# Linear attention and edge maps on one core: queries, keys and values in one pass over x, and plain heads divided in the projection out

## The chip, the cores and the metric

One NeuronCore of a Trainium2 chip runs the whole program in one launch. The metric is the device time in microseconds (us) from start to end. The engines are TensorE (PE, matmuls; its weight loads are PEld), VectorE (DVE), ScalarE (ACT), GpSimd (POOL) and SyncE (SP). Transfers run on 16 DMA engines, and are issued by SP's queue and by POOL's queue, each in order. On-chip memory is SBUF (128 partitions) and PSUM, which holds matmul results in eight banks of 128 x 512 float32.

## What is computed

Two layers on x of 4 images x 512 channels x 64 x 64 points, all in float32. The first is a linear attention over 64 heads of 8 channels, on the plain projections and again on their convolved copy:

```python
def layer0(x):                                     # cut to what matters
    q, k, v = h @ wq.T, h @ wk.T, h @ wv.T         # h: x with channels last
    qkv = ...                                      # per head 8 q, 8 k, 8 v channels
    dw = conv5x5_depthwise(qkv); pw = conv1x1_grouped(dw)
    qkv_all = concatenate([qkv, pw], axis=1)       # 64 plain heads, 64 convolved ones
    query, key_ = relu(f[:, :, :d]), relu(f[:, :, d:2*d])
    value_pad = concatenate([value, ones])         # the ones make the denominator
    scores = einsum('bhdn,bhen->bhde', value_pad, key_)
    out = einsum('bhde,bhen->bhdn', scores, query)
    out = out[:, :, :-1] / (out[:, :, -1:] + EPS)
    y = conv1x1(out, proj_kernel)                  # 1024 -> 512 channels
    return batch_norm(y) + x
```

The second takes four edge maps of its input with 3x3 kernels (Sobel, Laplace, diagonal, gradient), mixes each with a 512 -> 128 matmul, batch norm and GELU, weighs the 512 channels by a small attention over their means, mixes them 512 -> 512, applies a layer norm over channels and GELU, and adds its input.

## The kernel before

**Groups and strips.** The first layer goes through 16 groups: 4 images (b) x 4 groups (g) of 128 channels. An image's points are 8 strips of 512, in two halves of four. `load_x` (L265) brings a strip in two pieces of 512 KB on SP's queue; image 0 stays in SBUF, from image 1 on a group takes the strips from a pool of 8 pieces (`xst`).

**Two passes.** `keys_and_values` projects keys (`project`, L274) and values (`values`, L305) strip by strip, turns the keys (`turn`, L331) and sums the scores (`scores`, L342, added up on DVE in `s_sb`, L350). `queries` then reads the strips again, from the two that are still there, and projects the queries. `project` copies the result on ACT (`strip`, L283) and, for keys and queries, stores it from POOL's queue to a DRAM buffer `flat` (L288), of which there are two per kind; for queries ACT also makes `rq`, the relu (L281).

**Plain heads.** For each half of a group `denominators` multiplies `rq` with the key sums (`den`, L387), `invert` makes the reciprocal on DVE (`rec`, L380 and L381), `spread_out` spreads it over the channels with four matmuls into four banks (`over`, L396), and `divide` multiplies on DVE (L404) and stores `heads` to DRAM (SP).

**Convolved heads.** `roll` brings `flat` back with its rows rearranged (`rolled`, L295, POOL's queue, into one buffer). `convolve` (L418) makes a half's 5x5 convolution with 160 matmul instructions into four banks, 80 into the first two and then 80 into the others; ACT reads the banks, for keys in two pieces each, with relu and a sum (L431), for queries whole (L437). `conv_turn` (L445, L447) turns the convolved keys. `correlate` (L473) multiplies them with shifted values that are read back from DRAM (`near`: stored in `values`, L318, loaded by `load_near`, L458, into three buffers); four calls 0 to 3 fill two banks, and `weigh` (DVE, L491, L492), called at the end of the last, empties them. `conv_denominators` (`cden`, L565), `spread_out` and `conv_divide` (L574) end in `cheads` in DRAM. What of this a group doesn't reach in its own passes is done in the next group's first pass.

**PSUM.** Eight banks in two kinds of four: `ps_tile` (projections, values, turns, denominators, `yps`) and `quad_tiles` (convolution, correlation, `over`), each taken in the order in which the program asks.

**The image behind.** Three stages of the previous image run between the steps of the current one: Y (`project_out`), which reads `hd` (the plain heads of a strip, 1 MB, L656) and four `chd` (convolved heads, 256 KB each, L660), both on SP's queue, multiplies both with folded weights (`yps`, L676, first the four products with `hd`, then those with `chd`), adds shift and x (`yt`, L681) and stores `y`; E (`edge_branches`), with the edge maps on DVE, ACT and POOL and the matmuls `br` (L753); and F (`fuse_out`, `zps`, L865). `advance` hands each step of a pass a share of them, by hand-set shares and a pace. After the last group come a tail of its remaining steps with shares of their own, and then the last image's stages ("left").

PE's order is the program's; the other engines' orders are made by a scheduler from the same program.

Of the kernel before, what the change touches and what calls it, by code (L numbers as in the profile page):

```python
# [50 lines left out]
KV_ORDER = (1, 0, 2, 3, 4, 5, 6, 7)  # L51
Q_ORDER = (6, 7, 5, 4, 3, 2, 1, 0)
# [28 lines left out]
WORK, VALS = 18, 3  # L81
# [8 lines left out]
def conv_seq_kernel(  # L90
# [11 lines left out]
    xst = front.enter_context(tc.tile_pool(name="xst", bufs=8))  # L102
# [30 lines left out]
    def const_col(name, value):  # L133
# [12 lines left out]
    flats = {  # L146
        (t, n): dram.tile([4, P, NB, W], F32, name=f"flat{t}{n}", bufs=1) for t in (KEY, QUERY) for n in range(2)
    }

    def flat_border(n):  # L150

        for t in (KEY, QUERY):
            for r in range(4):
                nc.gpsimd.dma_start(out=flats[t, n][r, :, 0 if r < 2 else NB - 1, :], in_=zero_row[:, 0, 0:W])
# [64 lines left out]
    zero_row = const.tile([P, NCH, WB], F32, name="zero_row")  # L219
# [10 lines left out]

    class Group:


        def __init__(self, b, heads, cheads, folded, g):
            self.b, self.heads, self.cheads, self.folded, self.g = b, heads, cheads, folded, g
            self.near_dram = near[(NG * b + g) % 2]
            self.w, self.mat = {}, {}
            self.strip, self.rq, self.held, self.conv, self.near, self.rolled = {}, {}, {}, {}, {}, {}
            self.flat = {t: flats[t, (NG * b + g) % 2] for t in (KEY, QUERY)}
            self.nears = iter([(half, jp, b) for half in range(2) for jp in range(2) for b in range(2)])  # L240
# [3 lines left out]
        def load_w(self, t):  # L244
            self.w[t] = gw.tile([P, NCH, P], F32, name="w_sb", tag="w_sb", bufs=3)
            nc.sync.dma_start(out=self.w[t], in_=wqkv[self.g, t])
# [13 lines left out]
        def load_x(self, j):  # L260
            xs[self.b, j] = []
            for n in range(2):
                pool = x_first if self.b == 0 and j not in Q_ORDER[:2] else xst
# [4 lines left out]
        def project(self, t, j):  # L268
# [8 lines left out]
            if t == QUERY and (self.g == NG - 1 or self.b and j not in KV_ORDER[:2]):  # L277
                del xs[self.b, j]
            if t == QUERY:
                self.rq[j] = work_tile("rq")  # L280
                nc.scalar.activation(self.rq[j], ps, AF.Relu)  # L281
# [18 lines left out]
        def values(self, j):  # L300
# [8 lines left out]
            if self.b and j not in Q_ORDER[:2]:  # L309
                del xs[self.b, j]  # L310
            vt = vts[KV_ORDER.index(j) % 3]
# [16 lines left out]
        def turn(self, j):  # L328
# [5 lines left out]
            self.held[j] = kt, vts[KV_ORDER.index(j) % 3]  # L334
            del self.strip[j]

        def scores(self, j):
# [8 lines left out]
            if j == KV_ORDER[0]:  # L346
# [4 lines left out]
            if j == KV_ORDER[-1]:  # L351
                self.ks = mini.tile([P, 32], F32, name="ks_sb")
# [25 lines left out]
        def invert(self, den):  # L378
            rec = work_tile("rec")
            nc.vector.tensor_scalar(rec, den, ATT_EPS, None, ALU.add)  # L380
            nc.vector.reciprocal(rec, rec)  # L381
            return rec

        def denominators(self, half):
            den = ps_tile("den")
            for k in range(4):
                nc.tensor.matmul(  # L387
                    den[32 * k : 32 * k + 32, :], lhsT=self.ks, rhs=self.rq[4 * half + k], start=True, stop=True
                )
            self.rec = self.invert(den)  # L390

# [6 lines left out]

        def divide(self, half):
            banks = self.spread_out(self.rec)  # L400
            for k in range(4):
                j = 4 * half + k
                q = work_tile("q")
                nc.vector.tensor_mul(q, self.rq.pop(j), banks[k])  # L404
                nc.sync.dma_start(out=self.heads[j, :, self.g, :], in_=q)
# [170 lines left out]

        def keys_and_values(self, before):

# [558 lines left out]
```

## Time and profile before

| | us |
|---|---|
| three runs | 4784.38 median, 4782.71 to 4795.94 |
| the profiled execution | 4783.19, its span 4781.4 |
| PE busy in image 0's groups (0 to 840) | 806.67 |
| PE busy from 840 to 4080 | 3078.29 of 3240 |
| PE busy in the tail and the last image's stages (4080 to 4781) | 623.67 of 701 |
| mean granted clock of PE in the three stretches | 0.99, 0.98, 0.93 |
| DMA busy share in the three stretches | 0.82, 0.79, 0.53 |
| bytes moved | 997.96 MB, mean 209 GB/s |

The profile is one execution. The page gives each engine's busy time and a row of forty equal slices of the span (digits are tenths). The view of waits lists, for each line of an engine, how long the engine stood idle before it, and which instruction or transfer ended that: `yps L676 <- DMA chd` means that PE stood before a product of line 676 until a chd load had landed. Windows give the busy time of each engine between two times, with PE's granted clock (1.00 is full) and the share of time for which the 16 DMA engines were busy. The timeline lists the instructions of an engine in order of time, with the idle time before each.

The costliest transfers of the page (count, KB each, median us from issue to landing): x 316 x 512, 7.5; near loads 256 x 528, 9.6; rolled 512 x 256, 7.1; flat 256 x 256, 5.9; heads 128 x 256, 5.4; chd 128 x 256, 8.3; hd 32 x 1024, 7.7.

### The profile page before, as it was taken

To read this page: it belongs to the slowest core of one execution; us is meant where nothing else is said; L and a number is where in the kernel's file an instruction comes from. 1 tells how busy PE (TensorE), PEld (TensorE's weight loads), DVE (VectorE), ACT (ScalarE), POOL (GpSimd) and SP (SyncE) were. 2 spreads that over 40 slices of the span, in tenths; PEclk is the share of its full clock that TensorE was granted. 3 is DMA by queue.
4 is the path that set the end of the run, shared out by engine and by line. 5 is a ranking of instruction groups with operands and counts; after the bars stand their busy time and mean duration, and the time that the engine had idled before them with its cause. 6 is when DMAs were issued, how large, how long until landed. Compare 5 with 4: busy or idle time off the path is not lost. (4 is left out here: it accounts for less than half of the span.)

```text
span 4781.4 us, 85619 instructions
## 1 busy us (share of the span) xinstructions
PE 4508.6 (94%) x35900; PEld 2454.5 (51%) x35900; DVE 2102.4 (44%) x2788; ACT 1589.2 (33%) x2719; POOL 986.1 (21%) x1291
## 2 busy tenths in 40 slices
PE   8999999998999999989999999998999999899987
PEld 5555554444656554444465656453446565434433
DVE  1222222114666624311356654441125667347966
ACT  2122121002555423300244453430014545214765
POOL 2111111111121123211112121441111211111443
PEclk9999999999999999999999999999999999999998
DMA  9777799757898977877589888679668887655435
GB/s 258 176 181 193 184 257 255 180 158 196 230 248 230 264 220 216 241 185 193 166 227 259 225 259 238 213 228 226 168 187 235 236 239 202 206 161 152 152 129 174
DMA packets 466289, 997.96 MB, mean 209 GB/s; under 512 B 185544, under 2 KB 218344, under 8 KB 443376
## 3 DMA queue, kind: packets, MB, share of 16 engines
q1 hardware_dynamic: 383728, 722.41, 54.4%
q0 software_dynamic: 82176, 270.07, 20.6%
q8 instruction: 283, 4.64, 0.4%
q14 instruction: 102, 0.84, 0.1%
HBM read 710.67 MB, written 281.61 MB: 208 GB/s over the span
## 5 line engine op out<-in xcount | busy, mean ns | idle before, releaser
L274 PE MATMUL proj<-xt,w_sb 128*128 128x512 f32 x2048 | 947.1, 606 | 20.7 <-DVE s_sb L350 9.6
L274 PEld LDWEIGHTS proj<-xt,w_sb 128*128 128x128 f32 x2048 | 379.7, 193 | 507.9 <-issue 446.2
L418 PE MATMUL cv<-rolled,mat 64*32 64x504 f32 (+2 forms) x10240 | 574.5, 594 | 30.4 <-DMA rolled<-flat 14.1
L676 PE MATMUL yps<-chd,fold_sb 128*128 128x512 f32 x1024 | 470.8, 600 | 51.8 <-DMA chd<-cheads 51.7
L865 PE MATMUL zps<-ef,wf_sb 128*128 128x512 f32 (+1 forms) x1056 | 469.8, 598 | 28.5 <-ACT z L870 16.3
L305 PEld LDWEIGHTS val<-w_sb,xt 128*128 128x128 f32 x4096 | 469.7, 192 | 42.7 <-issue 29.5
L305 PE MATMUL val<-w_sb,xt 128*128 128x128 f32 x4096 | 484.9, 277 | 1.7 <-DVE vt L312 1.2
L676 PE MATMUL yps<-hd,fold_sb 128*128 128x512 f32 x1024 | 467.7, 600 | 10.1 <-DMA hd<-heads 8.5
L681 DVE SCALAR_TENSOR_TENSOR yt<-yps,shift,xr 128x512 f32<-128x512 f32 x128 | 95.7, 749 | 841.6 <-PE yps L676 726.4
L753 PE MATMUL br<-maps,wbr_sb 128*128 128x256 f32 (+1 forms) x1792 | 463.5, 412 | 0.0
L753 PEld LDWEIGHTS br<-maps,wbr_sb 128*128 128x128 f32 x1792 | 334.7, 189 | 137.4 <-issue 96.7
L418 PEld LDWEIGHTS cv<-rolled,mat 64*32 64x32 f32 x10240 | 196.9, 108 | 376.2 <-issue 353.7
L295 POOL DMA_DIRECT2D rolled<-flat x512 | 273.3, 538 | 537.3 <-PE cv L418 493.2
L288 POOL DMA_DIRECT2D flat<-strip x256 | 144.9, 566 | 1152.2 <-ACT strip L283 1117.9
L283 ACT COPY strip<-proj 128x512 f32<-128x512 f32 x256 | 149.1, 582 | 676.5 <-PE proj L274 676.3
L676 PEld LDWEIGHTS yps<-chd,fold_sb 128*128 128x128 f32 x1024 | 194.6, 192 | 304.6 <-issue 232.6
L473 PE MATMUL corr<-near,ckt 128*32 128x160 f32 x8192 | 331.9, 315 | 18.3 <-DMA near<-near 16.9
L865 PEld LDWEIGHTS zps<-ef,wf_sb 128*128 128x128 f32 x1056 | 203.6, 196 | 277.8 <-issue 226.5
L676 PEld LDWEIGHTS yps<-hd,fold_sb 128*128 128x128 f32 x1024 | 192.8, 192 | 248.9 <-issue 243.9
L473 PEld LDWEIGHTS corr<-near,ckt 128*32 128x32 f32 x8192 | 256.7, 111 | 114.2 <-issue 53.7
L685 POOL DMA_DIRECT2D y<-yt x128 | 114.4, 894 | 958.7 <-DVE yt L681 787.3
L729 DVE TENSOR_TENSOR maps<-dv 128x1054 f32<-128x1054 f32 (+1 forms) x112 | 159.9, 1428 | 257.0 <-PE br L753 256.9
(133 smaller groups left out, 4711.6 us busy)
## 6 DMA issues: line engine op xcount, KB each, us to landing
xt<-in_x SPq DMA_DIRECT2D x316, 512.0 KB, 7.5
near<-near SPq DMA_DIRECT2D x256, 528.0 KB, 9.6
rolled<-flat POOLq DMA_DIRECT2D x512, 256.0 KB, 7.1
flat<-strip POOLq DMA_DIRECT2D x256, 256.0 KB, 5.9
win<-y SPq DMA_DIRECT2D x96, 396.0 KB, 5.8
near<-vt SPq DMA_DIRECT2D x512, 66.0 KB, 5.6
y<-yt POOLq DMA_DIRECT2D x128, 264.0 KB, 6.1
heads<-q SPq DMA_DIRECT2D x128, 256.0 KB, 5.4
```

Of the source, the lines that this page charges most:

```text
L274: nc.tensor.matmul(ps, lhsT=self.w[t][:, c, :], rhs=xs[self.b, j][c], start=(c == 0), stop=(c == NCH - 1))
L283: nc.scalar.copy(s, ps)
L288: nc.gpsimd.dma_start(out=self.flat[t][r, :, b : b + 8, :], in_=rows(s))
L295: nc.gpsimd.dma_start(out=self.rolled[t, half][r::8, :, :], in_=self.flat[t][r % 4, :, at : at + 8, :].rearrange("(n c) b w -> c n (b w)", ...
L305: nc.tensor.matmul(ps[:, ts(c, P)], lhsT=xs[self.b, j][n][:, ts(c, P)], rhs=self.w[VALUE][:, n, :], start=(n == 0), stop=(n == NCH - 1),)
L418: nc.tensor.matmul(rows(banks[2 * s + i])[32 * j : 32 * j + 32, :, c0:c1], lhsT=self.mat[t][q, 4 * s + j, (dx + 2) * 4 : (dx + 2) * 4 + 4, :],
L473: nc.tensor.matmul(self.banks[jj][32 * i : 32 * i + 32, 160 * b : 160 * b + 160], lhsT=self.held["c", i][:, at : at + 32], rhs=v[:, 4 * n ...
L676: nc.tensor.matmul(ps, lhsT=fold_sb[g // NG][:, g % NG, ts(c, P)], rhs=hd[g], start=(g == 0), stop=(g == 2 * NG - 1),)
L685: nc.gpsimd.dma_start(out=y[c, :, at : at + 29 : 4, :], in_=yt)
L729: nc.vector.tensor_sub(flat[:, half : 3 * half - 2], dvs[:, 2 : 2 * half], dvs[:, 0 : 2 * half - 2])
L753: nc.tensor.matmul(rows(ps), lhsT=wbr_sb[:, k, c, :], rhs=rows(maps[:, slot[k], c % 2, :], WB)[:, :, 0:W], start=(c == 0), stop=(c == NCH ...
L865: nc.tensor.matmul(ps, lhsT=wf_sb[:, k, ts(c, P)], rhs=ef[k], start=(k == 0), stop=(k == 3))
```

## The change

**One pass.** `keys_and_values` and `queries` go. `steps` makes a group's 24 steps: for each strip the key projection, the value projection with its turn, and the query projection with its scores. The order of strips and of halves alternates with the group's parity, so that a group starts with the two strips that the one before ended with. All that a group needs beyond its projections, the two key convolutions included, is in `rest`, and is done in the next group's pass, at fixed steps. The previous image's stages are added at step 21 of the next image's first group; before, behind its first pass.

**Plain heads.** `rq`, `denominators`, `divide` and `heads` go. The queries' `flat` is kept for a whole image (two images in turn), and `project_out` loads `hd` from it, in rows of 2 KB instead of 8. `attend` makes, for the strip to come, the relus (ACT), the denominators of the four groups and their reciprocal, and two by two the spread and the product, with `over` in `ps` banks. The four products with `chd` go first. A strip's loads are issued before the products of the one before.

**Buffers.** Work tiles 18 to 16, x pieces 8 to 7, projection weights 3 to 6, `chd` 6 on the right and 4 for the last image's stages. The last group's remaining steps are `rest` with a table of shares, where step 8 stands before step 7.

```diff
-KV_ORDER = (1, 0, 2, 3, 4, 5, 6, 7)
-Q_ORDER = (6, 7, 5, 4, 3, 2, 1, 0)
+ORDERS = ((1, 0, 2, 3, 4, 5, 6, 7), (6, 7, 5, 4, 3, 2, 1, 0))
-WORK, VALS = 18, 3
+WORK, VALS = 16, 3
...
+    flat_k = [dram.tile([4, P, NB, W], F32, name=f"flatk{n}", bufs=1) for n in range(2)]
+    flat_q = [dram.tile([NG, 4, P, NB, W], F32, name=f"flatq{n}", bufs=1) for n in range(2)]
...
+            self.order, self.halves = ORDERS[g % 2], (g % 2, 1 - g % 2)
...
-            if t == QUERY:
-                self.rq[j] = work_tile("rq")
-                nc.scalar.activation(self.rq[j], ps, AF.Relu)
...
-        def denominators(self, half):
-            den = ps_tile("den")
-            for k in range(4):
-                nc.tensor.matmul(
-                    den[32 * k : 32 * k + 32, :], lhsT=self.ks, rhs=self.rq[4 * half + k], start=True, stop=True
-                )
-            self.rec = self.invert(den)
...
-        def divide(self, half):
-            banks = self.spread_out(self.rec)
-            for k in range(4):
-                j = 4 * half + k
-                q = work_tile("q")
-                nc.vector.tensor_mul(q, self.rq.pop(j), banks[k])
-                nc.sync.dma_start(out=self.heads[j, :, self.g, :], in_=q)
...
+            return {
+                1: [cv(KEY, h0), roll(KEY, h1)],
+                2: [*ct([(h0, 0), (h0, 1)]), own("fold_turn")],
+                3: ct([(h0, 2), (h0, 3)]),
+                4: [*co(h0, 0, 0), own("fold")],
+                5: co(h0, 0, 2),
+                6: co(h0, 1, 0),
+                7: [cv(KEY, h1), roll(QUERY, h0)],
+                8: co(h0, 1, 2),
+                9: [*ct([(h1, 0), (h1, 1)]), own("conv_sums")],
+                10: [*ct([(h1, 2), (h1, 3)]), own("load_pc", t=0.0)],
+                11: co(h1, 0, 0),
+                12: co(h1, 0, 2),
+                13: [cv(QUERY, h0), roll(QUERY, h1)],
+                14: co(h1, 1, 0),
+                15: [*co(h1, 1, 2), own("conv_denominators", h0), own("mix")],
+                16: [own("conv_weights")],
+                17: [own("conv_divide", h0), own("conv_heads")],
+                18: [cv(QUERY, h1), own("conv_fold")],
+                19: [own("conv_denominators", h1)],
+                21: [own("conv_divide", h1)],
+            }
...
+            own = {
+                8: [one(0.0, "load_mat", KEY)],
+                12: [(0.0, lambda: [following.load_w(t) for t in (KEY, VALUE, QUERY)])] if following else [],
+                16: [one(0.0, "load_wtab")],
+                19: [one(0.0, "load_mat", QUERY), one(0.0, "roll", KEY, self.halves[0])],
+                20: [one(0.0, "load_near", VALS)],
+            }
+            other = before.rest() if before else {}
+            if before and not self.g:
+                own[21] = [(0.0, lambda: behind.extend(stages(before)))]
+            seq = []
+            for i, j in enumerate(self.order):
+                for n, made in enumerate((
+                    [one(T_PROJ, "project", KEY, j)],
+                    [one(T_PROJ, "values", j), one(T_TURN, "turn", j)],
+                    [one(T_PROJ, "project", QUERY, j), one(T_SCORES, "scores", j)],
+                )):
+                    seq += made + other.get(3 * i + n, []) + own.get(3 * i + n, [])
+            return seq
...
+                r, at = (k + 2) % 4, 8 * half + (k + 2) // 4
+                q = pool.tile([P, NG, 512], F32, name="hd", tag="hd", bufs=2)
+                nc.sync.dma_start(
+                    out=q, in_=flat_q[b % 2][:, r, :, at : at + 8, :].rearrange("g p b w -> p g (b w)")
+                )
+                hd = [q[:, g, :] for g in range(NG)]
-                    t = pool.tile([P, 512], F32, name="chd", tag="chd", bufs=6)
+                    t = pool.tile([P, 512], F32, name="chd", tag="chd", bufs=6 if side == "right" else 4)
...
+            def attend(hd, part):
+                if part == 0:
+                    for g in range(NG):
+                        nc.scalar.activation(hd[g], hd[g], AF.Relu)
+                    den = ps_tile("den")
+                    for g in range(NG):
+                        nc.tensor.matmul(den[32 * g : 32 * g + 32, :], lhsT=ks[g], rhs=hd[g], start=True, stop=True)
+                    recs[:] = [pool.tile([P, 512], F32, name="hrec", tag="hrec")]
+                    invert(recs[0], den)
+                    return
+                for g in (2 * part - 2, 2 * part - 1):
+                    q = slice(32 * g, 32 * g + 32)
+                    over = ps_tile("over")
+                    nc.tensor.matmul(over, lhsT=spread[q, :], rhs=recs[0][q, :], start=True, stop=True)
+                    nc.vector.tensor_mul(hd[g], hd[g], over)
+            recs = []
+            following = load(0)
+            yield 0.7 * WAIT_Y
+            attend(following, 0)
+            yield 0.2 * WAIT_Y
+            attend(following, 1)
+            attend(following, 2)
+            yield 0.1 * WAIT_Y
...
+                hd = following
+                following = load(j + 1) if j + 1 < NJ else None
...
-                    for g in range(2 * NG):
+                    for n in range(2 * NG):
+                        g = (n + NG) % (2 * NG)
                         nc.tensor.matmul(
                             ps, lhsT=fold_sb[g // NG][:, g % NG, ts(c, P)], rhs=hd[g],
-                            start=(g == 0), stop=(g == 2 * NG - 1),
+                            start=(n == 0), stop=(n == 2 * NG - 1),
                         )
+                    if following and c:
+                        attend(following, c - 1)
...
+    tail = [
+        (1, (4.0, 0.0)), (2, (2.0, 2.0, 2.0)), (3, (2.0, 2.0)), (4, (1.0, 1.0, 1.0)), (5, (1.0, 1.0)), (6, (1.0, 1.0)),
+        (8, (1.0, 1.0)), (7, (4.0, 0.0)), (9, (2.0, 2.0, 2.0)), (10, (2.0, 2.0, 0.0)), (11, (1.0, 1.0)), (12, (1.0, 1.0)),
+        (13, (4.0, 0.0)), (14, (1.0, 1.0)), (15, (1.0, 1.0, 2.0, 2.0)), (16, (3.0,)), (17, (3.0, 3.0)), (18, (6.0, 3.0)),
+        (19, (10.0,)), (21, (4.0,)),
+    ]
```

## The prediction

> **What bounds the kernel now.** I read the page's busy times first, then the waits of TensorE (PE), then windows of busy time around the longest wait, then ScalarE's (ACT's) timeline behind a convolution.
>
> ```profile
> PE 4508.6 (94%) x35900; PEld 2454.5 (51%) x35900; DVE 2102.4 (44%) x2788; ACT 1589.2 (33%) x2719; POOL 986.1 (21%) x1291
> ...
> PEclk9999999999999999999999999999999999999998
> DMA  9777799757898977877589888679668887655435
> ```
>
> PE is busy 4508.6 of 4781.4 us. No other engine is near its limit over the span, and only idle PE time (273 us) and time at a lowered clock can be won. The waits of PE say what the idle time is made of:
>
> ```profile
> PE yps L676 <- DMA chd<-cheads: 51.7, 13, 22.0
> PE over L396 <- DVE rec L381: 17.2, 13, 5.3
> PE corr L473 <- DMA near<-near: 16.9, 5, 4.3
> ...
> PE cv L418 <- DMA rolled<-flat: 14.1, 4, 7.2
> PE ctr L445 <- ACT co L431: 13.3, 5, 5.0
> PE proj L274 <- DVE s_sb L350: 9.6, 2, 8.9
> PE cden L565 <- ACT strip L283: 8.9, 2, 7.9
> PE yps L676 <- DMA hd<-heads: 8.5, 1, 8.5
> ...
> PE fold L371 <- DMA p<-in_proj: 6.0, 1, 6.0
> ```
>
> The columns are the total, the number of waits and the longest. Transfers (chd, near, rolled, hd, p) make 97.2 us of it, and no single cause the most. The longest wait is seen in windows (length, busy times, granted clock, DMA share, GB/s):
>
> ```profile
> 3230.00:3270.00 40.00, 40.00 (x255) 17.89 (x240) 3.10 (x5) 3.35 (x6) 8.41 (x13) 1.00 1.03 262
> ...
> 3285.00:3300.00 15.00, 0.23 (x1) 0.24 (x2) 0.00 (x0) 0.00 (x0) 0.00 (x0) 0.50 1.02 240
> 3300.00:3305.00 5.00, 5.00 (x10) 2.22 (x11) 0.94 (x2) 0.00 (x0) 0.64 (x1) 0.71 1.01 216
> ```
>
> The DMA engines are full (share 1.03) for 40 us before PE stops: chd stands behind other transfers. The clock then is 0.50 and comes back late. So a long wait costs more than itself: after one of 3.60 us a convolution took 10.35 us in place of 8.65, after one of 8.46 us eight projection matmuls took 6.47 in place of 3.60, after one of 6.91 us sixteen took 10.16 in place of 7.03. That is 1.7, 2.9 and 3.1, a mean of 2.6 us a wait of some 3 us or more; short ones cost only themselves.
>
> Last, how long a convolution's results wait for ACT:
>
> ```profile
> 2415.31 8.65 PE L418 MATMUL cv<-rolled,mat 64*32 64x512 f32 x160
> ...
> 2430.68 1.17 ACT L749 ACTIVATE maps<-maps,sobel_eps 128x1048 f32<-128x1048 f32 x1 [1.57 <-DVE maps L748]
> 2431.75 0.36 ACT L431 ACTIVATE co<-cv 128x256 f32<-128x256 f32 x1
> ...
> 2433.08 0.22 ACT L431 ACTIVATION_READ_ACCUMULATOR co<-cv 128x1 f32 x1
> ```
>
> The first half of this key convolution ends at 2419.6 (half of 8.65 after its start). Its two banks are read by L431 only behind an edge map's chain of ACT and DVE steps, until 2433.1: 13.5 us. The same reading over all 32 key convolutions: 21 times 1.6 us or less (ACT idle) and once 1.8; ten times more (3.9, 4.0, 6.8, 7.7, 8.4, 9.3, 10.7, 10.8, 12.3, 13.5, together 87). The mean is (21 x 1.6 + 1.8 + 87)/32 = 3.8 us. Today it costs nothing: the second half has its own two banks.
>
> **The change, part by part.** *PE's own work* stays: the 256 den (L387) and 512 over (L396) matmuls are moved, none is added. So busy time changes by 0.
>
> *Traffic.* x loads fall from 316 to 172 (each of the last three images 52 pieces in place of 100): 144 x 524 KB = 75.5 MB less; the 128 heads stores of 262 KB, 33.6 MB, go too. 998 becomes 889 MB, 11% less. SP has 272 issues fewer, and none left that waits for DVE's division (the heads stores); near's loads still stand on its queue behind hd and chd loads that wait for buffers, as before. hd is now read in 2 KB rows; flat and chd rows of that size move as many bytes a second as hd's 8 KB rows here (about 0.10 us for 2 KB against 0.42 for 8 KB on one engine), so I cost that at 0. If it were wrong, 32 loads of some 7.7 us would stretch, at worst double: +7.7 each behind the prefetch of a strip, whose PE work is 4 x 7.0 = 28 us and hides it.
>
> *One pass in place of two.* Convolutions come at steps 1, 7, 13, 18 of 24 instead of close in pairs. Counted along PE's instruction order, the work between two convolutions (the cover of one rolled load, one buffer) is at least 29 us instead of 20; for a near slot 30 instead of 9; between rec's matmul and over 7.3 instead of 3.6, where DVE's chain is 0.69 + 3.35 = 4.04. Rolled took up to 19 us to land, near 27. So outside the tail I take those waits off: rolled -12 of 14.1, near -13 of 16.9, over on rec -12 of 17.2, p -4 of 6.0. The small ACT and DVE ones whose cover was 1 to 2 us (s_sb 9.6, strip 8.9 and 3.9, ckt 3.4 and 3.1, rq 2.5: 31.4 in all) have two projections more between; -20. Bounds: all of these stay (0) or go (-86).
>
> *Y's loads.* hd and chd cost 60.2. Now a strip's loads are issued one strip earlier, hd is needed sooner (relu and den come before the products), and chd, with as many buffers as before (6), sooner too since its products go first. With 11% less traffic, a middle value: -25, bounds 0 and -60.
>
> *Clock.* Of the waits removed, by their counts and longest, about 15 are long: 15 x 2.6 = -39. Gains together: 12 + 13 + 12 + 4 + 20 + 25 + 39 = -125.
>
> *The split convolution.* In step 6 the correlation opens its two accumulating banks, and step 8 ends them (weigh, L491). The second key convolution stands between, in step 7. Of the four banks of its kind it finds two, so its second half waits until ACT has read the first half. That holds for 15 of 16 groups; in the last 8 stands before 7. The price of one is the time read above: 15 x 3.8 = 57, and 10/32 of 15, 5 long ones, x 2.6 = 13: +70. Bounds: all at 1.6 (+24), all at 13.5 with the clock (15 x 16.1 = +242). Behind the stopped half stand, on PE, correlation, turns and projections: everything.
>
> [...]
>
> *The division moved into Y.* For each strip ACT makes 4 relus (4 x 0.594), DVE 0.69 + 3.35 + 4 x 0.68 = 6.8 us, PE 4 dens (0.64) and 4 overs (0.66). The same work goes from the passes. In a Y phase a strip lasts over 28 us of PE time, so it is covered; at a Y's start den to over has only 3.4 us of cover and the loads come together with roll and near: 4 x 2 = +8 (0 to +25).
>
> *New short covers.* kt to scores 3.4 us (7 before) and strip to turn 3.6; ACT's answers in the edge phases take over 3.4 us about one time in ten: +10 (0 to +30).
>
> *Tail.* Three den-over pairs stand next to each other, at 4.3 us each against 2.1 + 5.3 before: +6. Near, and chd with 4 buffers in place of 6: +4. Three of the new waits are long: +8. The last image's 8 x 6.8 = 54 us of DVE fall in Y's stretch (4200 to 4300), where DVE was busy 55 of 100; if they slid into 4410 to 4560, where it was busy 149.5 of 150, they would show in full.
>
> Losses: 70 + 8 + 10 + 6 + 4 + 8 = +106. **Sum: -19** on 4783.19, the profiled execution's own time (span 4781.4), 1.2 under the median: 4764 + 1 = **4765**.
>
> **The rivals.** (B) *Slower: the split waits behind edge maps.* In the changed kernel's ACT order, the evacuation stands behind an edge-map chain in 5 of the 15 groups, behind gelu or relu steps or a z in 6, behind nothing in 4. If all 11 pay the mean of the long ones (87/10 = 8.7): 96 + 4 x 1.6 = 102, and 11 x 2.6 = 29, 131 in place of 70: 4826. It decides from a mean wait of about 5 us, (57 + 19)/15. For it: the ten long rows above all lie where edge maps run. Against: 22 of 32 were free.
>
> (C) *Large gain.* ACT is free at the splits (24, no clock: -46), and hd and chd never wait (-35, five long ones -13): 4671. For it: the 22 us stall is one of full DMA. Against: outside that stall chd waited in 12 smaller places too.
>
> (D) *The transfers' volume was not the cause.* Y's loads come in a burst behind their own few buffers, whatever x does; hd and chd save nothing (+25 + 13): 4803. For it: chd's buffers are as many and its need earlier. Against: the DMA share of 1.03.
>
> **How the numbers follow.** Forecast 0.30 (own range 4735 to 4785), B 0.28, C 0.17, D 0.15; the rest between. No change (within 0.3%, 14 us, about what a measurement here can tell) lies between forecast and D: 0.10. Faster: most of the forecast's and C's cases, 0.47; slower: B's and D's, 0.43. The range goes from near C, 4680, past B to 4850, leaving out a still dearer split.
>
> **What would show it.** Waits of cv on ACT's co, about 15, totalling near 57: the split; over 100: B. Near, rolled and over on rec near zero before the tail: the single pass; their staying would undo 37 us. yps on chd and hd near 35: the forecast; near 0, C; 60, D. DMA traffic near 889 MB and PE busy within 15 us of 4508 plus the clock's part. Wrong would be a busy PE that grows by much more, or a wait at a place not named here.

## The result and the profile after

The changed kernel takes 4865.06 us (median; 4860.5 to 4870.1), the kernel before 4783.55 beside it: ratio 1.0166, 95% interval 1.0145 to 1.0187. It is slower by 1.7%, above the stated range of 4680 to 4850. Its profiled execution has a span of 4868.3 us, 86.9 more than before. Of the page:

```profile
PE 4546.5 (93%) x35900; PEld 2482.4 (51%) x35900; DVE 2108.4 (43%) x2788; ACT 1607.6 (33%) x2729; POOL 986.5 (20%) x1291
...
DMA packets 439533, 889.64 MB, mean 183 GB/s; under 512 B 181192, under 2 KB 213992, under 8 KB 420720
```

The bytes fell to 889.64 MB, as reckoned. But PE is busy 37.9 us longer with the same 35900 instructions, and idle 321.8 instead of 272.8 us: 49.0 more. (Idle is the span less PE's busy time.) The waits of PE in the changed kernel (total, number, longest):

```profile
PE cv L397 <- ACT co L410: 53.4, 15, 12.8
PE den L668 <- ACT hd L665: 40.6, 2, 25.0
PE val L308 <- ACT strip L286: 18.6, 2, 17.0
PE s L343 <- DVE vt L313: 16.9, 2, 14.6
...
PE over L675 <- DVE hrec L234: 11.9, 3, 7.0
PE corr L452 <- ACT co L416: 11.6, 2, 7.3
PE s L343 <- DVE cst L515: 9.8, 1, 9.8
PE st L364 <- ACT strip L286: 9.3, 3, 7.4
PE fold L372 <- DMA p<-in_proj: 8.7, 3, 4.0
...
PE over L383 <- DVE rec L234: 7.5, 1, 7.5
...
PE corr L452 <- DMA near<-near: 4.2, 1, 4.2
```

Nearly all waits on transfers are gone by name: yps on chd and hd (60.2 before) is 0, rolled is not in the list at all, near fell from 16.9 to 4.2. Those on p (8.7, before 6.0) and on the first load of x (5.4) stay. In the others' place stand waits on ACT and DVE. Three of them need a closer look.

**The split convolution.** Timeline of PE and ACT (start, length, engine, line, operation):

```profile
1261.83 4.44 PE L397 MATMUL cv<-rolled,mat 64*32 64x512 f32 x80
1279.09 6.89 PE L397 MATMUL cv<-rolled,mat 64*32 64x512 f32 x80 [12.82 <-ACT co L410]
...
1277.14 1.17 ACT L771 ACTIVATE maps<-maps,sobel_eps 128x1048 f32<-128x1048 f32 x1
1278.21 0.36 ACT L410 ACTIVATE co<-cv 128x256 f32<-128x256 f32 x1
```

The first 80 instructions end at 1266.3. ACT works through an edge map until 1278.2 and only then reads the banks that the second half needs. That half comes at a lowered clock (granted 0.69 over its time, 1.00 over the first half's): 6.89 us instead of 4.44.

**A wait that only looks like ACT's.** PE waits 17.0 us for a strip's copy on ACT. The same stretch on both engines:

```profile
3241.43 3.70 PE L280 MATMUL proj<-xt,w_sb 128*128 128x512 f32 x8
...
3263.13 4.10 PE L308 MATMUL val<-w_sb,xt 128*128 128x128 f32 x20 [17.00 <-ACT strip L286]
...
3260.94 1.67 ACT L665 ACTIVATE hd<-hd 128x512 f32<-128x512 f32 x3 [21.58 <-DMA hd<-flatq]
3262.52 0.56 ACT L286 COPY strip<-proj 128x512 f32<-128x512 f32 x1
```

ACT itself was idle for 21.58 us. The relu of `hd` stood at the head of its queue and waited for a 1 MB load, issued at 3239.2. The copy that PE needed, of a projection that ended at 3245.1, stood behind it. Such a load also explains the 25.0 us of den at the start of image 1's Y, but there it is only part of the wait: PE stood from 2006.8, the load was issued at 2020.3, behind two stores of F's results and the load of the folded weights on SP's queue, and the relu began at 2031.15. So 13.5 of the 25.0 us passed before the load was even asked for (and 4.4 of the 15.5 us at the last image's Y). The wait on hd's transfer did not go; it moved from yps to den, and through ACT's queue to work that has nothing to do with Y. den on hd and val on strip make 59.2 us, where chd and hd had cost 60.2; with over on hrec, which waits for DVE's reciprocal behind the denominators, it is 71.1. The Trainium skill ("TensorE: Matmul & The Clock Gate", Architectural detail) says that ScalarE's and VectorE's queues are strictly first in, first out; this trace agrees, with 21.58 us of an idle ACT in front of a ready copy.

**PE's own work.** Before, then after, one strip's or half's overs:

```profile
2448.27 1.14 PE L396 MATMUL over<-rec,consts_sb 32*128 32x512 f32 x8
```

```profile
2118.56 1.13 PE L675 MATMUL over<-hrec,consts_sb 32*128 32x512 f32 x4
...
2126.68 1.13 PE L675 MATMUL over<-hrec,consts_sb 32*128 32x512 f32 x4
```

Eight instructions (four matmuls of 32 rows) take 1.14 us when they follow each other; four take 1.13, as long. The first four of the eight start within 0.02 us of each other, so they run side by side, and the change takes them apart: in 28 of the 32 strips they come as two groups of four. 28 x 1.13 = 32 us more of PE. Counted from the records, by how far each carries PE's end on, over took 73.2 us before and 104.4 after: +31 of the 38 us of busy time. ("Packing small matmuls", Part 3 of the same page of the Trainium skill, gives 3.07 times for four row tiles at once; here two tiles cost as much as four.)

### The profile page after: what moved, and what is told of

Same layout as the page of the kernel before. It is cut to its first block, busy times and chain, and to the rows that moved or that the text cites. A ratio compares the mean times of both kernels' runs of the same rounds, so it can differ in the third digit from the quotient of the medians.

```text
span 4868.3 us, 85156 instructions
## 1 busy us (share of the span) xinstructions
PE 4546.5 (93%) x35900; PEld 2482.4 (51%) x35900; DVE 2108.4 (43%) x2788; ACT 1607.6 (33%) x2729; POOL 986.5 (20%) x1291
## 2 busy tenths in 40 slices
DMA packets 439533, 889.64 MB, mean 183 GB/s; under 512 B 181192, under 2 KB 213992, under 8 KB 420720
## 3 DMA queue, kind: packets, MB, share of 16 engines
q1 hardware_dynamic: 356848, 613.34, 46.6%
## 5 line engine op out<-in xcount | busy, mean ns | idle before, releaser
L280 PE MATMUL proj<-xt,w_sb 128*128 128x512 f32 x2048 | 957.8, 611 | 10.5 <-DMA xt<-in_x 5.4
L397 PE MATMUL cv<-rolled,mat 64*32 64x504 f32 (+2 forms) x10240 | 577.1, 590 | 54.6 <-ACT co L410 53.4
L452 PE MATMUL corr<-near,ckt 128*32 128x160 f32 x8192 | 341.4, 316 | 19.4 <-ACT co L416 11.6
L452 PEld LDWEIGHTS corr<-near,ckt 128*32 128x32 f32 x8192 | 268.9, 111 | 90.2 <-issue 53.5
L313 DVE COPY vt<-val 128x512 f32<-128x512 f32 x128 | 87.2, 682 | 394.6 <-PE val L308 364.8
L665 ACT ACTIVATE hd<-hd 128x512 f32<-128x512 f32 x128 | 70.8, 618 | 540.5 <-DMA hd<-flatq 468.7
```

The source lines that it names most:

```text
L280: nc.tensor.matmul(ps, lhsT=self.w[t][:, c, :], rhs=xs[self.b, j][c], start=(c == 0), stop=(c == NCH - 1))
L313: nc.vector.tensor_copy(vt.rearrange("p c q d -> p (c q) d")[:, :, 0:32], ps.rearrange("p (a d) -> p a d", d=32))
L397: nc.tensor.matmul(rows(banks[2 * s + i])[32 * j : 32 * j + 32, :, c0:c1], lhsT=self.mat[t][q, 4 * s + j, (dx + 2) * 4 : (dx + 2) * 4 + 4, :],
L452: nc.tensor.matmul(self.banks[jj][32 * i : 32 * i + 32, 160 * b : 160 * b + 160], lhsT=self.held["c", i][:, at : at + 32], rhs=v[:, 4 * n ...
```

## The experiments

They ran on three chips: e1 to e4 on chip 15, c0, e5, e7, e8 and e13 to e15 on chip 11, b0, e9 to e11 and e16 to e18 on chip 3. There the kernel before took 4750 to 4756 us, and the changed one 4857.93 (chip 11), ratio 1.0226 (1.0209 to 1.0244). So ratios to the kernel before of the same series are compared; 0.1% is 4.75 us. (Expectations given as times, up to e4, go by the first series' 4784.)

### The two kernels themselves

> The kernel before itself, profiled on the chip of the experiments: 1.000; its waits on chd and hd in Y 40 to 80 us, the key convolutions without any wait on ACT. Theory N (this chip favours it, by shorter waits on transfers): idle time of PE some 30 us below the 273 of the first profile.

Measured: 1.0002 (0.9988 to 1.0016), span 4750.0, PE busy 4497.7, idle 252.3 against the first profile's 272.8. Waits of PE:

```profile
PE yps L676 <- DMA chd<-cheads: 39.8, 13, 15.5
...
PE corr L473 <- DMA near<-near: 13.8, 5, 5.1
...
PE cv L418 <- DMA rolled<-flat: 8.7, 3, 4.6
PE yps L676 <- DMA hd<-heads: 8.5, 1, 8.5
```

Theory N holds in direction, with 20 us instead of 30: the waits on these four transfers were 91.2 us in the first series and are 70.8 here.

> The changed kernel as it is, beside the next three, for their comparison: 1.4 to 1.9 per cent above the kernel before of the same chip.

Measured: 1.0226, a little above what was expected. The trace has the same waits (cv on co 53.2, den on hd 39.4, val on strip 15.7); the changed kernel has few waits on transfers left to be shortened, which fits that it is only 7 us below the first series where the kernel before beside it (4749.55) is 34 below.

### e1: the weigh first

```diff
-                7: [cv(KEY, h1), roll(QUERY, h0)],
-                8: co(h0, 1, 2),
+                7: co(h0, 1, 2),
+                8: [cv(KEY, h1), roll(QUERY, h0)],
```

> The last correlation of a half and its weigh (step 8) put before the second key convolution (step 7) in every group. Theory S (the split convolution costs what its waits show, 53.4 us in 15, and the lowered clock behind the long ones): the waits of cv on ACT's co vanish, and the time falls by 53 to 70, from 4865 to some 4800. Rival: the wait only changes its place, to cv on DVE's weigh, since DVE's queue in the edge phases is as long as ACT's: a fall of less than 25, 4840 or more.

Measured: 4803.52, ratio 1.0111 (1.0094 to 1.0128). Against 1.0226 that is 1.15%, 55 us (some 12 either way by the two intervals), for 53.2 us of waits. No wait of cv on co or on weighed is left. Theory S holds, the rival falls. But the first of the waits left is larger than before:

```profile
PE den L668 <- ACT hd L665: 62.9, 3, 24.8
```

Part of what one stall gives back, the next takes: between the two profiled executions PE's idle time fell by 39 us (310.0 to 271.1).

### e2 and e3: the first relu and denominators later

```diff
-            yield 0.7 * WAIT_Y
+            yield 1.3 * WAIT_Y
             attend(following, 0)
-            yield 0.2 * WAIT_Y
+            yield 0.4 * WAIT_Y
...
-    each = SHARE_Y + SHARE_E + SHARE_F + WAIT_Y + 2 * WAIT_E + WAIT_F + 6.0
+    each = SHARE_Y + SHARE_E + SHARE_F + 1.8 * WAIT_Y + 2 * WAIT_E + WAIT_F + 6.0
...
-    for _ in range(3):
+    next(projected)
+    for _ in range(2):
+        if len(behind) > 1 and next(behind[0], None) is None:
+            behind.pop(0)
         next(projected)
```

> The first relu and denominators of Y come 1.3 instead of 0.7 of WAIT_Y behind the loads, the first spreads 0.4 instead of 0.2, and at the start of the last image's Y a step of the image behind stands between them. Theory Y (hd is asked for too early, and its relu blocks ACT's queue for all that stand behind it): the waits of den on hd (40.6), of val on strip behind a blocked ACT (17.0) and of over on hrec (11.9) fall from 69 to 20 or less, and the time by 45 to 65, to some 4810. Rival: the loads are late whatever is done (they stand behind the last image's F in SP's queue), and chd's products wait in their place: a fall below 20, 4845 or more.

Measured: 4815.92, ratio 1.0139 (1.0124 to 1.0154): 0.87%, 41 us less than the changed kernel, just under theory Y's 45 to 65. But the waits didn't do what theory Y said: den on hd 37.0 and val on strip 19.8 are as before. What fell is cv on co, to 33.3, and s on vt, to 6.1. The edit also raises `each`, the work of an image from which the pace of the stages behind is reckoned, so that all their steps shift; that other steps thus met ACT and DVE at other moments is likely, but not shown. The gain is real, its reason was not the one given.

> Both edits together. If the two losses are independent, the falls add up: 100 to 130, some 4745, below the time before. If one hides behind the other (a stall lets late work catch up), less than 80: 4785 or more.

Measured: 4770.15, ratio 1.0044 (1.0029 to 1.0059): 86 us less, against 96 for the sum of the two: between the two expectations, nearly additive, and not below the time before. den on hd (35.0) and val on strip (23.0) remain.

### e4: the division alone

Two passes as before, only the plain division moved into Y, with `flat_q`, `project_out` and `attend` of the changed kernel, and 16 work tiles:

```diff
-                self.rq[j] = work_tile("rq")
-                nc.scalar.activation(self.rq[j], ps, AF.Relu)
...
-own("denominators", 1), own("fold_turn"), pj(4), own("divide", 1), pj(5),
+own("fold_turn"), pj(4), pj(5),
```

> The kernel before with two passes and its own order, and only the division of the plain heads moved into Y (queries from the convolution's flat copy, no heads, no rq). Theory Y puts the loss at the division there: Y's start as in the changed kernel, 60 to 90 us of waits where there were 60, no split of convolutions (0 waits of cv on co), near and rolled waits as before: 4800 to 4830. Rival, the one pass alone is the loss: 4775 to 4795.

Measured: 4773.61, ratio 1.0053 (1.0035 to 1.0071): the division alone makes the kernel 25 us slower. As a ratio that lies in theory Y's range (4800 to 4830 of 4783.55 are 1.0034 to 1.0097).

```profile
PE 4530.2 (95%) x35900; PEld 2462.3 (52%) x35900; DVE 2106.0 (44%) x2788; ACT 1600.5 (34%) x2723; POOL 989.1 (21%) x1291
...
PE den L656 <- ACT hd L653: 36.7, 3, 13.9
PE corr L452 <- DMA near<-near: 20.9, 8, 4.7
PE cv L397 <- DMA rolled<-flatq: 16.5, 4, 7.7
```

Near and rolled wait as ever, though 33.6 MB of heads stores and their 128 issues are gone. So it is the one pass, not the lighter traffic of the division, that ends these waits. But the loss is not one of waits: beside b0_before, whose profiled execution is 17 us shorter, PE is idle 15.5 us less here (236.8 to 252.3) and busy 32.5 us more, and the overs, taken apart by the division's new place, make 31 of these (103.2 us of PE time to 72.3).

### e5: still later

```diff
-            yield 1.3 * WAIT_Y
+            yield 2.2 * WAIT_Y
...
-    each = SHARE_Y + SHARE_E + SHARE_F + 1.8 * WAIT_Y + 2 * WAIT_E + WAIT_F + 6.0
+    each = SHARE_Y + SHARE_E + SHARE_F + 2.7 * WAIT_Y + 2 * WAIT_E + WAIT_F + 6.0
```

> Both edits of e3, with the first relu and denominators still later: 2.2 of WAIT_Y behind Y's loads. Theory P (only the place of the first denominators in PE's order is wrong; the loads land some 22 us too late for it): the waits of den on hd (35.0) and of val on strip (23.0) fall together below 20, and the time lies 30 to 50 below e3's: 0.996 to 0.998 of before. Rival: Y's loads are always late, because they stand on SP's queue behind the last stores of F, which stand behind near's stores and loads; later dens only push the rest of the image behind: within 15 us of e3, 1.002 to 1.006.

Measured: 4797.3, ratio 1.0099 (1.0079 to 1.0119): worse than e3 by 0.55%, outside both expectations. den on hd fell to 14.0, but val on strip rose to 48.2. ACT's timeline in image 1 shows why:

```profile
2024.12 2.19 ACT L665 ACTIVATE hd<-hd 128x512 f32<-128x512 f32 x4 [27.86 <-DMA hd<-flatq]
2026.21 0.56 ACT L286 COPY strip<-proj 128x512 f32<-128x512 f32 x1
```

This is the second strip's relu, whose load was issued at 2004.4. PE's order is written by hand, ACT's is not: there the relu is placed as if its load had landed, before the strip's copy. Later denominators on PE leave it there, and ACT is idle for 27.86 us. This corrects theory P: the place of den in PE's order was not the only wrong one.

### e7: as many bytes as before

```diff
             nc.gpsimd.dma_start(out=self.flat[t][r, :, b : b + 8, :], in_=rows(s))
+            for _ in range(2 if self.b else 0):
+                spare = dram.tile([P, 512], F32, name="spare", bufs=16)
+                nc.gpsimd.dma_start(out=spare, in_=s)
```

> The changed kernel, with each key and query strip of the last three images also stored twice into scratch from POOL's queue: 384 x 262 KB = 101 MB more, as many bytes as before the change. Theory V (the waits on transfers went because there is less traffic): waits of corr on near, of cv on rolled and of yps on chd come back, 30 us or more in all, and the time grows by 30 to 80. Rival O (they went because the order gives each transfer more work to hide behind): these three stay below 15 us together, the time grows by less than 20.

Measured: 990.36 MB, 4875.33, ratio 1.0263 (1.0246 to 1.0280): 0.37%, 17 us more. Of near, rolled and chd one wait is left:

```profile
PE corr L455 <- DMA near<-near: 4.4, 1, 4.4
```

Rival O holds for these three: 11% of the traffic is worth 17 us or less here (POOL's extra issues are in it). Some of it shows at hd: den on hd is 45.2 and val on strip 19.0, together 9 us more than in c0. That the waits went because the order gives each transfer more work to hide behind is what is left of the two theories, not shown by itself: the bytes came back on POOL's queue, and SP's queue keeps its 272 issues fewer, which no run parts from the order (e4, with 128 of them gone, has near's waits still).

### e8: F's stores on POOL's queue

```diff
-                    nc.sync.dma_start(out=out[b, c, :, 512 * j + first : 512 * j + end], in_=z)
+                    (nc.sync if b == B - 1 else nc.gpsimd).dma_start(
+                        out=out[b, c, :, 512 * j + first : 512 * j + end], in_=z
+                    )
```

> Both edits of e3, and the stores of F's results (out) of the first three images are issued from POOL's queue, right behind the addition that makes them, not from SP's. Theory Q (Y's start is late because F's last stores stand on SP's queue behind near's, and hold the memory that hd's loads need): hd is asked for 10 to 20 us sooner after F's last matmul, den on hd and val on strip (58 together) fall below 25, and the time lies 25 to 45 below e3's. Rival: the load's own 11 to 23 us under full DMA are what is waited for: within 15 us of e3.

Measured: 4796.97, ratio 1.0095 (1.0078 to 1.0112), 24 us worse than e3. den on hd (32.7) and val on strip (20.4) stay, and a new wait comes, var on POOL's total, 27.0. hd is asked for 7 and 8 us sooner (39.8 and 13.3 us behind F's last matmul in images 1 and 2, in e3 46.6 and 21.4), but from there to its first relu it takes 17.4 and 29.1 us instead of 12.5 and 22.7. So theory Q's gain does not come: what the earlier issue wins, the longer load takes. The DMA share was 0.97 and 1.03 in the two stretches of e3 in which its loads were under way (1953 to 1975, 3141 to 3164), which is the rival's reason; in time the run lies outside both expectations, and var's new wait (8.0 in e3) takes 19 of the 24 us. In image 1 of e3 PE stood 9.1 of its 22.3 us before the load was issued; e8 brings that down to 2.0 of 20.1, and the load takes the rest.

### e9, e10, e11: relus on POOL

```diff
-                        nc.scalar.activation(hd[g], hd[g], AF.Relu)
+                        nc.gpsimd.tensor_scalar(hd[g], hd[g], 0.0, None, ALU.max)
```

> Both edits of e3, and all relus of hd made on POOL instead of ACT. Theory A (a relu that waits for hd's transfer stands in ACT's queue in front of the evacuations that PE needs): val on strip (23.0) goes, as do the other waits on ACT behind hd; den on hd stays at 30 to 40, now for POOL; 15 to 35 us below e3: 0.997 to 1.001. Rival: POOL then stands still before flat stores, rolled loads and F's sums, and PE waits there as long: 1.003 or more.

Measured: 4761.6, ratio 1.0021 (1.0011 to 1.0031), 11 us below e3 (the two intervals touch): less than theory A gave, more than its rival. The waits decide: val on strip (23.0 in e3) is gone altogether. The first wait is now

```profile
PE den L668 <- POOL hd L665: 46.8, 5, 23.1
```

Theory A holds for the mechanism: here POOL bears the wait for the load without holding up work that PE needs. den still waits for the load itself, and longer than in e3 (35.0): of the 58.0 us of the two waits 46.8 are left.

> The later first denominators of e5 (2.2 of WAIT_Y), and the relus on POOL. Theory A: in e5 the wait had only moved from den to val on strip (48.2), since ACT stood before the relu all the same; with the relu off ACT both are gone, Y's start costs below 20 in front of the tail, 45 to 65 below e5: 0.996 to 1.001. Rival: as for e9; 1.004 or more.

Measured: 1.0042 (1.0028 to 1.0056), 27 us below e5, at the rival's bound. den on hd is down to 15.4 and val on strip to 2.2, as theory A has it, but a wait of proj on x (24.2, in e5 5.0) comes in their place, and ksum on DVE stays as in e5 (17.2).

```diff
-LEFT_E = 14.0
+LEFT_E = 44.0
...
-    for _ in range(2):
+    for n in range(6):
         if len(behind) > 1 and next(behind[0], None) is None:
             behind.pop(0)
-        next(projected)
+        if n in (3, 5):
+            next(projected)
```

> e10 with LEFT_E 44 instead of 14 (more of image 2's edge stage is left for the end), and four steps of it in front of the last image's first denominators and two behind them, instead of one and one. Theory T (the tail's den on hd 14, over on hrec 4 and the overs on rec are waits without work to fill them): 15 to 25 below e10. Rival: the edge stage there is held by DVE and ACT itself, and the filling waits for maps: within 8 us of e10.

Measured: 1.0102 (1.0084 to 1.0120), 0.6% worse than e10. The tail's waits on hd are gone from the head of the list, but LEFT_E shifts the whole interleaving, and new ones appear in front (hid on watt 29.0, fold on p 16.1, cv on flat 14.1). Neither expectation foresaw that; the edit changed more than the tail.

### e13 to e16: the overs side by side

```diff
-                for g in (2 * part - 2, 2 * part - 1):
-                    ...
+                overs = [ps_tile("over") for _ in range(NG)]
+                for g in range(NG):
+                    q = slice(32 * g, 32 * g + 32)
+                    nc.tensor.matmul(overs[g], lhsT=spread[q, :], rhs=recs[0][q, :], start=True, stop=True)
...
```

> The changed kernel with one edit: a strip's four overs in Y one behind the other into four banks, instead of two and two in separate steps. Theory R (four matmuls of 32 rows each run side by side on PE, so that two and two take twice the time: over took 104 us of PE in all, against 72 before): over falls by some 30 us of PE time, and the time by 20 to 35, from 1.0226 to 1.015 to 1.018. Rival: the 30 us lie in cold stretches or in the accounting, or the four banks make the next projections wait: within 10 us, 1.020 or more.

Measured: 1.0219 (1.0201 to 1.0238), against 1.0226: no difference. But the overs weren't side by side:

```profile
2069.93 2.03 PE L677 MATMUL over<-hrec,consts_sb 32*128 32x512 f32 x8
```

Three start together and the fourth 0.9 us later, as it takes the bank of the product just made, which DVE must empty first. Over's PE time is 102.0 instead of 104.4, so this run doesn't decide theory R.

> e9 (weigh first, later first denominators, relus on POOL) with the four overs together. If the four losses named (split, relu on ACT, place of the first denominators, overs in pairs) are all there is, the one pass's gain shows: 0.994 to 0.998 of before. Rival: another loss is left, the last group's work in the tail above all: 0.999 or more.

Measured: 4756.07, ratio 1.0010 (0.9998 to 1.0022): no difference from the kernel before, as the rival has it. Something else is left.

> e4 (the two passes of before, the division in Y) with relus on POOL and the four overs together. If the moved division by itself costs nothing once these two are mended: 0.997 to 1.001, against 1.0053 of e4. If it lies below e14, the one pass has no gain of its own.

Measured: 1.0070 (1.0051 to 1.0089): not mended, and not to be told from e4. den on POOL's hd 39.8, near 19.4, rolled 17.1. The overs were not mended either: with the fourth coming alone as in e13 they take 99.5 us of PE, after 103.2 in e4. e14 is 0.6%, 28 us, better, with one pass in place of two; but it also has the later first denominators, which e15 lacks, so the 28 us are not the one pass's alone.

> e14 with the four overs of a strip in the four banks of the convolution's kind instead of the projections' kind, where the fourth stood behind the evacuation of the product just made, and so came alone, 0.9 us later. Theory R: all four run side by side, over falls from 98 to about 70 us of PE time, and the time by 20 to 30 from 1.001: 0.995 to 0.997. Rival: the convolutions and correlations, which use these banks, now wait for DVE's products: 1.000 or more.

The edit takes `quad_tiles("over")` for the four banks. Measured: 1.0000 (0.9986 to 1.0013). The overs of 26 of the 32 strips now come together, as before the change:

```profile
2014.22 1.14 PE L677 MATMUL over<-hrec,consts_sb 32*128 32x512 f32 x8
2055.11 1.13 PE L677 MATMUL over<-hrec,consts_sb 32*128 32x512 f32 x4
2057.07 2.36 PE L677 MATMUL over<-hrec,consts_sb 32*128 32x512 f32 x4 [0.83 <-DVE hd L679]
```

Over's PE time fell from 98.5 in e14 to 86.1 us, and some sets are parted by a wait for DVE. Theory R is shown for PE's time; in the total the gain is 5 us, within the intervals, as the rival has it.

### e17 and e18: the tail's order

```diff
+    others[14], others[15] = others[14] + others[15][:2], others[15][2:]
...
-        (13, (4.0, 0.0)), (14, (1.0, 1.0)), (15, (1.0, 1.0, 2.0, 2.0)), (16, (3.0,)), (17, (3.0, 3.0)), (18, (6.0, 3.0)),
+        (14, (1.0, 1.0, 1.0, 1.0)), (13, (4.0, 0.0)), (15, (2.0, 2.0)), (16, (3.0,)), (17, (3.0, 3.0)), (18, (6.0, 3.0)),
```

> e14 with the last group's correlations all in front of its first query convolution. Theory T: corr on co in the tail (8 to 11 us, a correlation that waits for ACT to empty the convolution's banks) goes, with the clock behind it: 8 to 15 us, 0.998 to 0.9995. Rival: the denominators behind the convolution wait in its place: 1.000 or more.

Measured: 1.0006 (0.9991 to 1.0020), not to be told from e14. corr on co fell from 10.9 to 2.8, and cden on co rose from 13.2 to 18.8 and over on rec from 7.5 to 11.8: the rival.

> e16 and e17 together: if both theories hold, 30 to 40 below e14, 0.992 to 0.995, and so below the kernel before.

Measured: 4746.65, ratio 0.9992 (0.9978 to 1.0005). It is the fastest of the variants, 2.3% below the changed kernel, and not distinguishable from the kernel before. It differs from e17, run beside it on the same chip, in the overs' banks alone: over took 99.0 us of PE in e17 and 85.1 here, PE was busy 4521.6 and 4510.7, and the medians of twelve runs each are 4754.87 and 4746.65. So 14 us of overs are worth 8 us of time (1.6 to 13.8 when the runs are resampled).

## Why the prediction was wrong

The forecast was 4765 from a sum of -19; the span grew by 86.9, of it 49.0 idle and 37.9 busy time of PE. Term by term, by the trace of the changed kernel and the runs (the rows are not a full account of the 86.9):

| term of the sum | predicted | measured |
|---|---|---|
| near, rolled | -25, in the tail +4 | 31.0 became 4.2 (near, at the tail): -26.8 in waits |
| over on rec, before the tail | -12 | 11.9 became 0 |
| over on rec, in the tail | +6 | 5.3 became 12.7 (rec, cstw): +7.4 |
| p | -4 | 6.0 became 8.7: +2.7 |
| small waits on ACT and DVE by name | -20 | 31.4 became under 2: about -30; corr and cden on co, 18.1, are new |
| Y's loads and its start | -25 and +8 | chd and hd -60.2, den, val and hrec +71.1: +10.9 |
| the split convolutions | +57, with the clock +70 | +53.4 in waits; 55 us of time (e1) |
| PE's own work | 0 | over +31 us of busy time |
| new short covers | +10 | s on vt and cst, st on strip alone 36.0 |
| clock | -39, and +13 and +8 for new long waits | busy time without over +7; granted mean 0.973 before, 0.967 after |

**Right**, in size: near and rolled, over on rec, and the split, 15 times, at a mean of 3.6 us against 3.8, with single waits up to 12.8 behind edge maps. For the split the mechanism is shown too (e1); for near and rolled the order is what e4 and e7 leave as the likelier cause. Rival B's 4826 came nearest to 4865 by luck: its price of the split (131 us) was not reached. Rival D had the term of Y's loads right: they saved nothing. But it too looked for them at yps. By the prediction's own sign (yps on chd and hd near 0) the trace would have been rival C's large gain; the wait had only changed its name.

**The steps that failed.** First, "Y's loads: a middle value: -25", with the division "so it is covered". The two terms were to give 17 us and cost 10.9. The relu was costed by ACT's busy time (4 x 0.594), not by what is queued behind it while it waits for a load. The loads' wait did not shrink with 11% less traffic, and e7, with the bytes back, adds only 9 us to it: volume was not its main cause. e5 and e9 show what it did to ACT: with den later, the wait appears at val; with the relu off ACT, it is gone from there, and 46.8 us are left at den. Part of these pass before the load is issued, part while it is under way; no run takes them off.

Second, "PE's own work stays". The count of matmuls stayed, their neighbours did not. (Of the 512 overs only 256 are moved; the others are the convolved heads'.) The price was in the rows all along: eight over instructions in 1.14 us, whose single ones last up to 0.69. The trace shows the +31 us of PE time; e4 shows them as 31 of the 32.5 us that PE is busier by the moved division alone, with 25 us more time; e18 against e17 gives 14 of them back, for 8 us of time.

Third, the new short covers. They were priced by ACT's usual delay (+10). What came were three waits of 7 to 15 us near the starts of the edge stage (9.8, 14.6 and 7.4, in three images): two when DVE had 13 to 14 us of work, most of it for maps, in front of a values copy, the third behind ACT's steps for maps. e3 removes part of that (s on vt from 14.9 to 6.4, s on cst from 13.2 to 0), without an edit that aimed at it, so their cause is argued, not shown.

Fourth, the clock: the sum took 15 long waits off and added 8; counted in the traces, without the first load of x, waits of 2.5 us and more went from 30 (165 us) to 35 (241 us).

**Still open.** e18 undoes the split, the relu on ACT and most of the parted overs. It has 209 us of gaps between PE's records against 229 in the kernel before (b0_before), but 13 us more of busy time and no gain that the runs can tell. As much as these 13 us is what its overs still take more (85.1 us to 72.3). Its den still waits 47.2 us for hd, of which PE stands 9.3 us in image 1 before the load is issued, and from the last projection on it has 84 us of gaps instead of 69. Whether an issue of hd early enough would make the one pass pay was not tried; e8, the one run that asked for it some us sooner, gained nothing by that. Nor was a version tried in which all overs come together, in one pass or in two.

## What to carry to other kernels

When a step is moved to another stage, ask on which queue its wait will stand, and what stands behind it there: a cheap instruction that waits for a load can stop an engine that has nothing to do with that load. Count a group of small matmuls as a group: here four of 32 rows cost as much as two, and taking them apart doubled them. Follow a wait that a change is to remove to the instruction that will need the same load next: the sign that it is gone has to name that place too. And when a buffer kind has four banks and a step wants four, look for every accumulation that is open across it in the order of instructions; that was the part of this forecast that held.

## What the runs showed of the hardware that was not expected

The kernel before took 4783.55 us in the series of the result, and 4749.55 to 4756.14 in the five series of the experiments, on three chips. The chip of the first series is not on record, so that the difference of some 30 us lies in the chip is likely but not shown. Between the two profiled executions (first series and b0_before) the span differs by 31.4 us: 20.5 of idle time, as much as the waits on four transfers (91.2 and 70.8), and 10.9 of busy time (4508.6 and 4497.7). The changed kernel, with few such waits, was 7 us apart (4865.06 and 4857.93). A ratio of two kernels of which one waits on transfers can thus differ between series by more than its own interval: 1.0166 and 1.0226.
